# First X spreads on ScalarE's queue, and the offset-weight sums moved behind the first norm's root

## The chip, the cores and the metric

The kernel runs on one core of a Trainium2 chip. The metric is the device time of one execution in microseconds, the median of several runs. TensorE (PE) multiplies into PSUM, VectorE (DVE), ScalarE (ACT) and GpSimd (POOL) do the elementwise work, and SyncE (SP) issues nearly all transfers. All data are 32-bit floats. In the tables of the profile a product of 32-bit floats appears as two matmul instructions.

## The reference, cut to what matters

Two layers follow each other. Layer 0 is a residual bottleneck with three convolutions and batch norms over 64 images of 1024 channels, 14 by 14. Layer 1, where the change lies, is a deformable bottleneck:

```
a   = relu(group_norm(conv1x1(x, w1)))          # 1024 -> 256 channels ("first norm")
om  = conv3x3(a, w_off) + b_off                 # 27 channels: 9 x-offsets, 9 y-offsets, 9 masks
s   = bilinear_sample(a, grid + offsets) * sigmoid(mask)   # 9 taps
h   = relu(group_norm(einsum(s, w2)))
out = relu(group_norm(conv1x1(h, w3)) + x)
```

## The kernel before

**Pairs.** Layer 1 works on 32 pairs of images; a pair is one row of 392 pixels for each channel. The stages of neighbouring pairs are interleaved so that TensorE always has a product to run. `fill` (L2188) opens the layer with the first three pairs, `slot` (L1971) goes on from there, `steady` runs pairs 2 to 29 and `tail` ends it.

**Sampling as products.** The bilinear weights of an output pixel split into a factor along rows and a factor along columns. Both are computed on 126 partitions (9 taps by 14 positions) by `factors` (L1362), stored to a small DRAM tensor `wd`, and read back by transfers that repeat them: `spread_rows` (L1441) brings S, `spread_columns` (L1456) brings X, each to 126 partitions (9 image rows by 14 columns). `corners` (L1500) multiplies S by X on DVE at L1511. The product is the matrix that `sampling` (L1515) multiplies with the transposed activations `aT` at L1531. ACT copies each result from PSUM at L1539. The nine taps are split in two sets, e = 0 with five and e = 1 with four, and each set in three pieces of output rows, so a pair has six S transfers and six X transfers. `lend` (L1414) copies parts of `aT` by two more transfers.

**The opening.** The steps of `fill` are, in the order written: the first convolution of pair 0; that of pair 1 with the first norm of pair 0, `offset_weights` (L879, which makes four sums and differences of the offset weights from `goff` in DVE instructions at L883 to L888), the offset convolution of pair 0 (L1300) and `selection(0)` (L1333, which brings the offsets to the 126 partitions) among it; the transposes of pair 0; the statistics of pair 1's norm, the residual of pair 2 and `factors(0)`; the step `spread` (six S, six X and the two lends of pair 0); and then the first convolution of pair 2 (L1151), with the scale of pair 1's norm, its four relus on ACT (L1235), pair 1's shifted sums (`transform`, L1276), `sums_of_second(0, 3)` (eight DVE instructions at L916), `corners(0, 0)` and pair 1's offset convolution among it. TensorE's order is exactly that order.

**What orders the other engines.** In the opening only TensorE's order is fixed by hand. The order of DVE, ACT, POOL and SP is made by the framework's planner, which takes the ready instruction that was written first, by its own idea of the times. An instruction wrapped in `tc.keep_in_program_order` stays behind the instruction that was written just before it *for the same engine*; this ties order alone and adds no wait for a result. The first norm is three steps: `mean`, `root` (its last instruction is a power on POOL, L1062, after DVE's L1061) and `scale` (DVE, L1078 to L1085, the first of them tied). The relus of a first norm (L1235), the sums at L916 and the corners at L1511 are tied too. A transfer counts as an instruction of the engine that issues it. The framework also gives every transfer that SP or ACT issues one of eight completion semaphores in turn, and a transfer waits until the one before it on its semaphore has landed.

Of the kernel before, what the change touches and what calls it, by code (L numbers as in the profile page):

```python
# [12 lines left out]
ALU = mybir.AluOpType  # L13
# [31 lines left out]
def kernel(  # L45
# [18 lines left out]
    nc = tc.nc  # L64
# [814 lines left out]
    def offset_weights():  # L879
        g0, g1, g2 = (goff.rearrange("p (n k) o -> p n k o", k=3)[:, :, k] for k in range(3))  # L880
        w1, w0, w2, w3 = (woff_sb[:, n] for n in range(4))

        nc.vector.tensor_tensor(w0, g0, g2, ALU.add)  # L883
        nc.vector.tensor_scalar(w0, w0, 0.5, None, ALU.mult)
        nc.vector.scalar_tensor_tensor(w1, g1, 0.5, w0, ALU.mult, ALU.add)
        nc.vector.scalar_tensor_tensor(w2, g1, -0.5, w0, ALU.mult, ALU.add)
        nc.vector.tensor_scalar(w0, g0, -1.0, None, ALU.mult)
        nc.vector.tensor_copy(w3, g2)  # L888
# [41 lines left out]
    def build_second_bottleneck(l1, path, run, early):  # L930
# [160 lines left out]
        def start(p):  # L1091
            pairs[p] = {"y": Y[p % 4]}
# [189 lines left out]
        def offset_conv(p):  # L1282
            q = pairs[p]
            half = W // 2

            def step(n):

                c, k = divmod(n, 3)
                k = (1, 0, 2)[k]
                if n == 0:  # L1290

                    q["po"] = ps_d.tile([P, N2], FP, tag="pd0", name=f"om_{p}")[:, :HW].rearrange(
                        "p (i q) -> p i q", i=2
                    )
                u = room(p)

                o0, o1 = (half if k == 0 else 0), (H - 1 if k == 2 else H) * half
                i0 = o0 + (k - 1) * half
                for m in range(4):
                    nc.tensor.matmul(  # L1300
                        q["po"][ts(m, 32), :, o0:o1],
                        woff_sb[:, m, 3 * c + k, :],
                        u[:, c, (2, 0, 3, 1)[m], :, i0 : i0 + o1 - o0],
                        start=(n == 0),
                        stop=(n == 3 * MB - 1),
                    )
                if n == 3 * MB - 1:


                    om = one.tile([P, N2], FP, tag="om", name=f"om_{p}")[:32]  # L1310
                    q["sums"] = om[:, :HW], om[:, HW:]
                    even, odd = q["sums"]
                    m1, m2 = (q["po"][ts(m, 32)].rearrange("p i q -> p (i q)") for m in (0, 2))
                    nc.scalar.activation(even, m1, AF.Identity, bias=boff_sb[:32])
                    nc.vector.tensor_tensor(odd, even, m2, ALU.subtract)
                    nc.vector.tensor_tensor(even, even, m2, ALU.add)

            return [lambda n=n: step(n) for n in range(3 * MB)]
# [14 lines left out]
        def selection(p):  # L1333

            q = pairs[p]

            def step():

                if "om" not in q:
                    offsets(p)  # L1340
                om = q["om"]
                mask = one.tile([P, N2], FP, tag="om", name=f"mask_{p}")[:32]
                nc.scalar.activation(mask, om, AF.Sigmoid)
                dm = dbounce.tile([27, N2], FP, tag="dm", name=f"dm_{p}")
                nc.sync.dma_start(dm[:18], om[:18])
                nc.sync.dma_start(dm[18:], mask[18:27])
                nc.vector.tensor_reduce(
                    omax[:, p : p + 1],
                    om,
                    mybir.AxisListType.X,  # L1350
                    ALU.max,
                    apply_absolute_value=True,
                )

                wt = q["wt"] = one.tile([KY, 2, N2], FP, tag="wt", name=f"wt_{p}")
                mk = q["mk"] = one.tile([P, N2], FP, tag="om", name=f"mk_{p}")[:KY, :]
                for n, dst in ((1, wt[:, 0, :]), (0, wt[:, 1, :]), (2, mk)):
                    nc.sync.dma_start(dst, dm[ts(n, T)].unsqueeze(0).to_broadcast([H, T, N2]))

            return [step]  # L1360
# [76 lines left out]
        def sample_buffer(e, name):  # L1437
            t = one.tile([P, MB, KT[e % 2], 2, HW], FP, tag=f"sm{e % 2}", name=name)
            return t.rearrange("p c k i q -> p (c k i q)")

        def spread_rows(p, e):  # L1441

            q = pairs[p]
            k0, k1 = tapsets[e]
            S = one.tile([QR, wide * KT[e % 2]], FP, tag=f"S{e % 2}", name=f"S_{p}_{e}")
            q["S"][e] = S
            for g, r0, piece in pieces(e):
                yield nc.sync.dma_start(  # L1448
                    S[:, piece],
                    q["wd"][g][0, r0 : r0 + R, k0:k1, :]  # L1450
                    .rearrange("r k n -> r (k n)")
                    .unsqueeze(1)
                    .to_broadcast([R, W, piece.stop - piece.start]),
                )

        def spread_columns(p, e):  # L1456

            q = pairs[p]
            k0, k1 = tapsets[e]
            n = wide * KT[e % 2]  # L1460
            if shared and p < 2 and e == 0:


                first, second = (
                    one.tile([P, HB, N2], FP, tag=f"z{n}", name=f"X_{p}_{n}").rearrange("p b n -> p (b n)")
                    for n in range(2)
                )

                cut = [piece for _, _, piece in pieces(e)][-1].start
                where = lambda piece: (  # L1470
                    second[:QR, : piece.stop - cut] if piece.start == cut else first[:QR, piece]
                )

                if p == 0:
                    q["spare"] = second[:QR, wide * KT[0] - cut :]
            elif shared:
                t = sample_buffer(e, f"X_{p}_{e}")
                last = [piece for _, _, piece in pieces(e)][-1]
                spare = q.get("spare") if e == 1 else None
                where = lambda piece: (  # L1480
                    spare[:, : piece.stop - piece.start]
                    if spare is not None and piece == last
                    else t[:QR, piece]
                )
                if e == 1:
                    transformed[p + 1] = t[:, n:]
            else:
                t = one.tile([QR, n], FP, tag=f"X{e % 2}", name=f"X_{p}_{e}")
                where = lambda piece: t[:, piece]
            q["X"][e] = where  # L1490
            for g, r0, piece in pieces(e):
                yield nc.sync.dma_start(  # L1492
                    where(piece),
                    q["wd"][g][1, :, k0:k1, :]
                    .rearrange("r k n -> r (k n)")
                    .unsqueeze(0)
                    .to_broadcast([R, W, piece.stop - piece.start]),
                )
# [688 lines left out]
        def fill():  # L2187

            for p in range(3):
                start(p)  # L2190
            load_h3(2, Z0)
            steps = first_conv(0, by_inputs=True)
            norm = first_norm(0)
            steps += put(
                first_conv(1),
                norm[:3] + [offset_weights] + norm[3:] + offset_conv(0) + selection(0),
                (3, 3, 5, 5, 6, 6, 6, 6) + (12,) * (MB * 3) + (12,),
            )
            norm, (distances, end) = first_norm(1), factors(0)
            steps += [lambda: pairs[1]["gn1"].total(), lambda: residual(2, 0, 3)] + transposes(0)  # L2200

            steps += norm[:2] + [lambda: residual(2, 3, 7), distances, lambda: residual(2, 7), end]

            def spread():

                for e in range(2):
                    for n, _ in enumerate(zip(spread_rows(0, e), spread_columns(0, e))):
                        if e == n == 0:
                            lend(0)

            steps += [spread]
            steps += put(
                first_conv(2),
                norm[2:]
                + [lambda: sums_of_second(0, 3), lambda: corners(0, 0)]
                + offset_conv(1)
                + selection(1)
                + [lambda: sums_of_second(6)],
                (3, 7, 7, 8, 8, 11, 11) + (12,) * (MB * 3) + (14, 16),
            )  # L2220
            for step in steps:
                step()
# [106 lines left out]
```

## Time and profile before

| what | value |
|---|---|
| median of three runs | 2783.32 us (2782.42 to 2784.22) |
| the profiled execution | 2784.07 us, of which its span is 2782.3 us |
| busy share of the span | PE 98%, PEld 76%, DVE 85%, ACT 51%, POOL 39% |
| mean granted TensorE clock | 0.992 |
| layer 1 begins on TensorE | first L1151 matmul at 967.98 us |
| first sampling product, pair 0 | 1013.51 us |
| first product of pair 0's second convolution (L1643) | 1030.06 us |

Times are microseconds from the start of the span. In a row of the timeline the first number is the start, the second the time from there to the end of the group, then engine, line, operation, what is written and what is read, and the count; brackets give the idle time before it and what ended it. "SPq" is SP issuing a transfer: its time is the issue, not the movement of the data. Windows list the busy time of each engine in a stretch, then the granted clock, the busy share of the 16 DMA engines and the rate in GB/s.

### The profile page before, as it was taken

To read this page: it belongs to the slowest core of one execution; us is meant where nothing else is said; L and a number is where in the kernel's file an instruction comes from. 1 tells how busy PE (TensorE), PEld (TensorE's weight loads), DVE (VectorE), ACT (ScalarE), POOL (GpSimd) and SP (SyncE) were. 2 spreads that over 40 slices of the span, in tenths; PEclk is the share of its full clock that TensorE was granted. 3 is DMA by queue.
4 is the path that set the end of the run, shared out by engine and by line. 5 is a ranking of instruction groups with operands and counts; after the bars stand their busy time and mean duration, and the time that the engine had idled before them with its cause. 6 is when DMAs were issued, how large, how long until landed. Compare 5 with 4: busy or idle time off the path is not lost.

```text
span 2782.3 us, 41225 instructions
## 1 busy us (share of the span) xinstructions
PE 2717.7 (98%) x13626; PEld 2110.4 (76%) x13626; DVE 2378.3 (85%) x4856; ACT 1411.3 (51%) x2806; POOL 1092.5 (39%) x1210
## 2 busy tenths in 40 slices
PE   9999899998999989999999999999999999999997
PEld 5555555554555558889989998998899899989974
DVE  7877899998888878888888888888888888888876
ACT  0000212212555544667666767666666667576654
POOL 4631366663666402332333343333333332433221
PEclk9999999999999999999999999999999999999998
DMA  7666000002556445666757675766667666757641
GB/s 232 193 176 175 29 1 0 1 1 111 208 208 224 175 130 174 167 159 173 204 163 171 175 206 149 177 190 191 155 173 201 171 168 173 210 149 177 175 133 51
DMA packets 350324, 424.31 MB, mean 153 GB/s; under 512 B 27892, under 2 KB 292500, under 8 KB 349844
## 3 DMA queue, kind: packets, MB, share of 16 engines
q1 hardware_dynamic: 291860, 376.61, 41.3%
q0 software_dynamic: 58240, 44.96, 11.6%
q8 instruction: 110, 1.80, 0.3%
q14 instruction: 114, 0.93, 0.1%
HBM read 296.49 MB, written 116.76 MB: 149 GB/s over the span
## 4 chain that ended last, share of the span: by engine, by line
PE 56%; DVE 3%; issue 2%; DMA 2%; ACT 1%; POOL 1%; SPq 1%; ACTq 0%; DVEq 0%; POOLq 0%
PE pd L1643 21%; PE sp L1531 12%; PE d L1780 10%; PE d L1190 9%; PE om L1300 2%; DMA X<-wd 1%; PE tr L1407 1%; PE pd L1562 1%; DMA h<-in_x_dram 0%; DVE sm L1599 0%; DVE st L1013 0%; SPq L1492 0%; SPq L1448 0%; DVE h L1130 0%; DVE X L1276 0%
## 5 line engine op out<-in xcount | busy, mean ns | idle before, releaser
L1531 PE MATMUL sp<-S,aT 126*128 126x420 f32 (+3 forms) x1536 | 487.8, 416 | 7.6 <-DVE S L1511 5.2
L1643 PE MATMUL pd<-sm,w2b_sb 128*128 128x196 f32 x2232 | 400.9, 329 | 1.2 <-DVE sm L1599 1.2
L1539 ACT COPY sm<-sp 128x336 f32<-128x336 f32 (+3 forms) x640 | 283.6, 448 | 195.3 <-PE sp L1531 182.6
L1643 PEld LDWEIGHTS pd<-sm,w2b_sb 128*128 128x128 f32 x2232 | 369.6, 190 | 1.8 <-DVE sm L1599 1.8
L530 PE MATMUL c<-v,u_sb 128*128 128x392 f32 x1024 | 342.8, 497 | 11.0 <-DVE bn1sh L167 8.2
L530 PEld LDWEIGHTS c<-v,u_sb 128*128 128x128 f32 x1024 | 194.5, 191 | 159.3 <-issue 11.6
L1643 PE MATMUL pd<-sm,Sc 128*128 128x196 f32 x1674 | 303.4, 329 | 0.0
L1643 PEld LDWEIGHTS pd<-sm,Sc 128*128 128x128 f32 x1674 | 279.6, 190 | 0.2
L1599 DVE TENSOR_TENSOR sm<-sm 128x980 f32<-128x980 f32 (+2 forms) x257 | 265.2, 1051 | 12.6 <-PE pd L1643 8.8
L1531 PEld LDWEIGHTS sp<-S,aT 126*128 126x128 f32 x1536 | 259.4, 192 | 20.1 <-issue 9.5
L1867 ACT ACTIVATE z<-z,gn_0sh,gn_0sc 128x196 f32<-128x196 f32 x496 | 224.7, 536 | 12.5 <-DVE gn_0sh L1085 12.5
L1674 POOL TENSOR_TENSOR E<-V,E 128x196 f32<-128x196 f32 x31 | 18.7, 602 | 517.6 <-DVE V L1673 517.6
L516 DVE TENSOR_TENSOR v<-t 128x392 f32<-128x392 f32 x256 | 193.0, 812 | 0.0
L1780 PE MATMUL d<-h,w3b_sb 128*128 128x196 f32 x744 | 174.2, 330 | 1.6 <-ACT h L1695 1.6
L1190 PE MATMUL d<-h,w1b_sb 128*128 128x196 f32 x928 | 168.2, 329 | 1.1 <-DVE V L1206 1.1
L1780 PEld LDWEIGHTS d<-h,w3b_sb 128*128 128x128 f32 x744 | 133.0, 189 | 44.6 <-issue 18.9
L1190 PEld LDWEIGHTS d<-h,w1b_sb 128*128 128x128 f32 x928 | 155.9, 190 | 1.4 <-DVE V L1206 1.4
L385 PE MATMUL c<-xc,w1a_sb 128*128 128x392 f32 x384 | 149.1, 497 | 5.4 <-DMA xc<-in_x_dram 5.4
L1103 ACT ACTIVATE h<-h,bn3sh,bn3sc 128x392 f32<-128x392 f32 x224 | 150.0, 706 | 0.0
L1511 DVE TENSOR_TENSOR S<-S,X 126x840 f32<-126x840 f32 (+1 forms) x192 | 139.8, 767 | 9.3 <-DMA X<-wd 8.8
L504 POOL TENSOR_TENSOR t<-wpad 128x784 f32<-128x784 f32 x62 | 95.3, 1537 | 127.3 <-DVE v L516 127.3
L1792 POOL TENSOR_TENSOR E<-V,E 128x196 f32<-128x196 f32 x124 | 80.2, 647 | 159.1 <-ACT h L1103 111.3
(710 smaller groups left out, 5558.4 us busy)
## 6 DMA issues: line engine op xcount, KB each, us to landing
xc<-in_x_dram SPq DMA_DIRECT2D x128, 392.0 KB
h<-o SPq DMA_DIRECT2D x64, 784.0 KB
h<-h SPq DMA_DIRECT2D x64, 784.0 KB
out_dram<-z SPq DMA_DIRECT2D x124, 392.0 KB
h<-in_x_dram POOLq DMA_DIRECT2D x56, 784.0 KB, 12.2
X<-wd SPq DMA_DIRECT2D x64, 413.4 KB
S<-wd SPq DMA_DIRECT2D x64, 413.4 KB
S<-wd SPq DMA_DIRECT2D x64, 330.8 KB
```

What stands on the lines that cost most here:

```text
L385: nc.tensor.matmul(acc[m], a, b, start=(j == 0), stop=(j == HB - 1))
L516: nc.vector.tensor_tensor(v[:, u].rearrange("p (i y x) -> p i y x", y=7, x=7), cols[c][:, :, i : i + 13 : 2, :], cols[c][:, :, j : j + 13 ...
L530: nc.tensor.matmul(m[u], u_sb[:, c, u, k % 4, ts(o, P)], vts[k][c][:, u], start=(c == 0), stop=(c == MB - 1),)
L1103: nc.scalar.activation(y, y, AF.Identity, bias=bn3.sh[:, b : b + 1], scale=bn3.sc[:, b : b + 1])
L1190: nc.tensor.matmul(bank[:, m % 2 if m < 6 else 1], a[:, k], b[:, k], start=(k == 0 and m < 6), stop=(k == HB - 1), skip_group_check=True,)
L1511: nc.vector.tensor_tensor(S[:, piece], S[:, piece], X(piece), ALU.mult)
L1531: nc.tensor.matmul(pt[:, i], q["aT"][:, i0 + i, c, starts.index(r0), :], q["corner", e][g, r0][:, :, i0 + i, :], start=(j == 0), stop=(j = ...
L1539: nc.scalar.copy(dst, pt.rearrange("p i k n -> p k i n"))
L1599: return nc.vector.tensor_tensor(dst, a, b, ALU.subtract)
L1643: nc.tensor.matmul(bank[:, m % 2], a[:, k], b[:, k - k0],  start=(k == 0 and m in (5, 0, 2, 6)), stop=(k == T - 1), skip_group_check=True,)
L1780: nc.tensor.matmul(bank[:, m % 2 if m < 6 else 1], a, b, start=(m < 6), stop=True, skip_group_check=True)
L1867: nc.scalar.activation(z[:, ts(i, HW)], z[:, ts(i, HW)], AF.Identity, bias=n.sh[:, b, i : i + 1], scale=n.sc[:, b, i : i + 1],)
```

## The change

Two things in `fill` change; nothing else in the kernel is rewritten.

1. `spread_columns` gets a parameter for the queue, SP by default; `fill` passes ScalarE's. So the six X transfers of pair 0 are issued by ACT, and the six S transfers and the two lends stay on SP. The other 31 pairs keep all on SP.
2. `offset_weights` is written between `root` and `scale` of pair 0's first norm instead of after `scale`, and its first instruction (L883) is tied to that place by `keep_in_program_order`.

```diff
-        nc.vector.tensor_tensor(w0, g0, g2, ALU.add)
+        tc.keep_in_program_order(nc.vector.tensor_tensor(w0, g0, g2, ALU.add))
...
-        def spread_columns(p, e):
+        def spread_columns(p, e, queue=nc.sync):
...
-                yield nc.sync.dma_start(
+                yield queue.dma_start(
...
-                norm[:3] + [offset_weights] + norm[3:] + offset_conv(0) + selection(0),
+                norm[:2] + [offset_weights] + norm[2:] + offset_conv(0) + selection(0),
...
-                    for n, _ in enumerate(zip(spread_rows(0, e), spread_columns(0, e))):
+                    for n, _ in enumerate(zip(spread_rows(0, e), spread_columns(0, e, nc.scalar))):
```

## The prediction, made before the changed kernel was run

> **What bounds the kernel now.** I read the page's engine shares first, then windows over the opening, then the waits there, then the timeline of each engine. The page says that TensorE sets the time: what TensorE loses in the opening is lost at the end, since after 1030 us it hardly idles.
>
> ```profile
> PE 2717.7 (98%) x13626; PEld 2110.4 (76%) x13626; DVE 2378.3 (85%) x4856; ACT 1411.3 (51%) x2806; POOL 1092.5 (39%) x1210
> ```
>
> TensorE's own timeline, 1003 to 1031 us, shows the stretch that the change can move:
>
> ```profile
> 1003.42 3.56 PE L1151 MATMUL d<-h,w1b_sb 128*128 128x392 f32 x10 [0.57 <-ACT h L224]
> 1006.91 2.11 PE L1300 MATMUL om<-X,woff_sb 128*32 128x196 f32 x48
> 1008.95 2.90 PE L1151 MATMUL d<-h,w1b_sb 128*128 128x392 f32 x8
> 1013.51 4.04 PE L1531 MATMUL sp<-S,aT 126*128 126x420 f32 x16 [1.66 <-DVE S L1511]
> 1019.94 10.28 PE L1531 MATMUL sp<-S,aT 126*128 126x420 f32 x32 [2.40 <-DVE S L1511]
> ```
>
> Two gaps, 1.66 and 2.40 us, both waiting for corners. DVE's rows name what the corners waited for: the first came straight after the sums at L916 (their last row starts at 1011.51 and lasts 0.54) plus 0.37, the third for an X transfer.
>
> ```profile
> 1012.42 1.03 DVE L1511 TENSOR_TENSOR S<-S,X 126x840 f32<-126x840 f32 x1 [0.37 <-DMA S<-wd]
> ...
> 1018.76 1.03 DVE L1511 TENSOR_TENSOR S<-S,X 126x840 f32<-126x840 f32 x1 [1.80 <-DMA X<-wd]
> ```
>
> Three windows show the transfers' rate before and in the second gap, and the clock behind it:
>
> ```profile
> 1012.00:1017.60 5.60, 4.04 (x16) 2.53 (x16) 3.12 (x9) 2.41 (x5) 0.00 (x0) 1.00 0.59 217
> 1017.60:1019.90 2.30, 0.00 (x0) 0.00 (x0) 1.10 (x2) 0.00 (x0) 0.00 (x0) 1.00 0.58 223
> 1019.90:1023.70 3.80, 3.76 (x6) 1.70 (x7) 3.79 (x10) 2.05 (x5) 0.00 (x0) 0.55 0.59 227
> ```
>
> The rate stands near 220 GB/s (the column after the DMA share, 0.58) as long as S and X move. And the 2.3 us gap was followed by 3.8 us at clock 0.55, which stretched the eight matmuls of piece three from about 2.8 us (8 at 0.35 apart) to 4.4.
>
> SP's rows show whether issuing or moving is the limit:
>
> ```profile
> 1004.73 0.78 SPq L1492 DMA_DIRECT2D X<-wd  x1
> 1006.01 0.76 SPq L1448 DMA_DIRECT2D S<-wd  x1
> ...
> 1015.75 0.73 SPq L1492 DMA_DIRECT2D X<-wd  x1
> ```
>
> Issuing ends at 1016.5; the last X is used at 1025.43, after a wait. The six S and six X are 3.56 MB, the lends 0.26; at 220 GB/s that is 17.4 us, and traffic begins at 1007.0: it must end at 1024.4 whoever issues. Moving is the limit.
>
> Last, ACT, the new issuer, and SP's waits in the same stretch:
>
> ```profile
> 1002.76 0.61 ACT L224 ACTIVATE h<-h,bn3sh 128x392 f32<-128x392 f32 x1
> 1003.96 0.99 ACT L1235 ACTIVATE a<-a,gn_1sh,gn_1sc 128x196 f32<-128x196 f32 x2 [0.59 <-DVE gn_1sh L1085]
> ```
>
> ```profile
> SPq L1345 <- DMA S<-wd: 0.3, 1, 0.3
> ```
>
> The last row is a transfer (`dm`) that waits for an S it has nothing in common with: the rule of eight semaphores at work.
>
> **Part 1, the X transfers.** Removed: six issues of 0.74 us from SP. That is worth nothing by itself, since moving is the limit. Added: six issues on ACT, and a new order. In the order written, the last ACT instruction before pair 1's first relu (L1235) is now the sixth X. That relu is tied, so all four relus now queue behind six issues; with them wait `transform`, the offset convolution of pair 1 and all of TensorE behind it, and the sums at L916 and the corners, tied behind `transform` on DVE.
>
> An ACT-issued transfer is in no row. Nearest are SP's 0.73 to 0.78 for the same shape: I take 0.78. Bounds: 0.27 (the small `dm` issue at 1020.91) and 1.5 (each waiting out one of SP's); a gain is excluded, since it is added to a tied queue. X0 needs the `wd` store that released it at 1004.73; it can't go earlier except by part 2. Six in a row at 0.78 end at 1009.4.
>
> But the semaphores hold some back. The trace's mixed S and X order lets me suppose that the planner alternates the queues: X0 S0 X1 lend X2 lend X3 S1 X4 S2 X5. Then X4 waits for X0 to land and X5 for X1. By the half-microsecond slices of the transfer view X0 begins to move at 1007.0, 2.3 us after its issue, and has some 0.25 MB of its 0.42 across by 1008.3, when S0 joins and the 220 GB/s are halved: (0.17 + 0.14 MB)/0.11 MB per us = 2.8 us, so X1 is across at 1011.1 and lands about 0.8 later (S0 before: across between 1010.9 and 1012.2, landed by 1012.4). X5 then issues from 1011.9 to 1012.7. With part 2's 0.25 off, the relus start near 1012.45 instead of 1003.96: **8.5 late**.
>
> What follows: the sums end at 1012.05 + 8.5 = 1020.55, and the first sampling matmul comes 1.09 later (1012.42 to 1013.51): 1021.65. TensorE's side: the offset convolution idles from 1007 to about 1014.6, some 7.6 us, starts at the low clock, and with the four remaining steps ends about 1021.5, so the two meet. From there nothing is missing: S and X have all landed by some 1024.4, and the sampling runs unbroken at full clock: 4.04 + 2.82 + 5.6 (the 24 of the second set, 1024.4 to 1030.06) = 12.46. TensorE reaches L1643 at 1034.1 against 1030.06: **+4.05 us**. The low clock of before (1.6) and both gaps (4.06) are thereby given back; without that the loss would be 8.5. The next work of pair 1 (offsets to corners) has cover: its corners run at 1047.65 on DVE without a wait, and TensorE uses them at 1051.84.
>
> The Trainium skill (DMA: Bandwidth & Descriptors, Issuing engines are not separate DMA queues) says that issuing from several engines saves only the issue time, as all share the same 16 engines. It speaks against the change, and the 9.6 us between the last issue's start and its use agree: by the rule, part 1 without the queueing on ACT would be worth 0. The skill's Perfetto Trace Analysis (DMA Instruction — HWDGE) has the descriptor generator locked by one sequencer at a time; no row here shows two issuers, and by that rule alone, without the semaphores, the X issues would take turns with SP's and end near 1012.3, which by chance gives the same +4.
>
> **Part 2, the sums of the offset weights.** Six DVE instructions stood at 978.84 to 980.75, ahead of the statistics:
>
> ```profile
> 980.75 1.05 DVE L1013 BATCH_NORM_STATS2 st<-a 128x6 f32<-128x392 f32 x2
> ...
> 985.13 0.16 DVE L1078 SCALAR_TENSOR_TENSOR gn_0sc<-gn_0B,vec 128x4 f32<-128x4 f32 x1 [1.14 <-POOL gn_0B L1062]
> ```
>
> ACT's copies for the statistics start at 979.49 and take 0.85, so the statistics can start near 980.0 and end at 981.1 instead of 981.8: 0.7 gained. L883 to L887 go into the 1.14 us in which DVE waits for POOL's power; by their distances they take 0.27 + 0.27 + 0.28 + 0.38 + 0.37 = 1.57, so 0.45 sticks out. The copy at L888 depends on none of them and stays early; if it too came behind the root it would cost 0.34 more. Sum: −0.25, bounds −0.7 and +0.1. TensorE idled 0.71 before the offset convolution of pair 0 (987.86), so this is on the path down to X0's issue, and is in the 8.5 above.
>
> **Sum.** Profiled execution 2784.07 + 4.05 = 2788.1; that execution lies 0.75 above the median, so for the median 2783.32 + 4.05 = **2787.4 us**. A difference under 0.2% (5.57 us) is about what a measurement of this kernel can tell from no change, so the forecast is a small loss inside that bound.
>
> **Rivals.**
> - *Heavier hold (slower).* The sixth or fifth X gets the semaphore of S0 or a lend instead. S0 shares the rate and lands at 1012.8 to 1013.5, so the relus start at 1013.6 to 14.3 or, with issues of 1.5, near 1015: 2788.5 to 2790. It decides from a relu start of 1014, where the loss passes 5.57. For it: the `dm` row, and an alternation that I only infer. Against: X0 was ready before S0.
> - *Issues only.* No X is held: relus from 1009.2, 5.25 late; sampling from 1018.4, L1643 at 1030.85: +0.8, 2784.1. For it: if the planner sends all six before S0, they draw only on semaphores of old transfers. Even with issues of 0.27 the relus come at 1006.2, but then X3 to X5 take half the rate from S2, which lands near 1021 instead of 1018, and piece three starts near 1022: +0.6 to +2.
> - *Transfers win (faster).* Two queues raise the rate above 220 and the relus aren't late. The first corner can't precede the sums, so sampling starts at 1013.1 at best and runs unbroken: L1643 at 1025.6, −4.5, with part 2 −4.8: 2778.5 to 2783. Against it: the rate is flat while issues queue up ahead.
> - *No effect:* only part 2 shows, 2783.1.
>
> **How the numbers follow.** Forecast 0.55 (its own range 2785.8 to 2789.8, from the landing times and 0.6 to 1.1 per issue; some 0.4 of it beyond 2788.9), heavier hold 0.17 (three quarters beyond), issues only 0.20, transfers win 0.05, no effect 0.03. Slower by over 0.2%: 0.22 + 0.13 = 0.35. Faster: 0.04, since even the win stays inside and only a new planner order elsewhere could add to it. Within: 0.61. Range 2782.6 to 2791.4: below lie most of the win, above a hold with long issues.
>
> **What would show it.** Right: ACT's timeline has six X issues between 1004.5 and about 1012.5, with waits before the last two, and L1235 of pair 1 only then; TensorE idles some 7 us before the second L1300 group; the sampling then has no gap of over 0.5 us; the rate is still near 220. In part 2: L1078 with no wait for POOL, the statistics at 980.0. Wrong: relus near 1004 (the tie missed the transfer), a rate well above 220, or a gap before piece three.

## The result, and the profile after

| | median of runs | profiled execution (span) | mean clock |
|---|---|---|---|
| before | 2784.55 us (2782.11 to 2787.86, 17 runs) | 2784.07 (2782.3) | 0.992 |
| after | 2789.46 us (2786.94 to 2793.16, 17 runs) | 2789.37 (2787.6) | 0.991 |

The ratio is 1.0020, 95% interval 1.0013 to 1.0027: slower by 5.6 us (3.6 to 7.5). The prediction was 2787.4 in a range of 2782.6 to 2791.4, with "within 0.2%" as the likeliest sign. The measured loss stands at that bound.

The two profiled executions did not reach layer 1 at the same time. All positions below are therefore also given "shifted": less the difference in the start of layer 0's last twelve h updates (DVE, L213), which is 972.39 in before and 972.66 in after, so 0.27 for after.

The engine shares, on the page of the changed kernel:

```profile
PE 2719.5 (98%) x13626; PEld 2112.8 (76%) x13626; DVE 2377.9 (85%) x4856; ACT 1411.3 (51%) x2806; POOL 1093.2 (39%) x1210
```

They say nothing of the change; the opening does. TensorE's timeline there:

```profile
1003.53 3.56 PE L1151 MATMUL d<-h,w1b_sb 128*128 128x392 f32 x10 [0.93 <-ACT h L224]
1015.88 4.37 PE L1300 MATMUL om<-X,woff_sb 128*32 128x196 f32 x48 [8.79 <-DVE X L1276]
1020.18 3.60 PE L1151 MATMUL d<-h,w1b_sb 128*128 128x392 f32 x8
1023.62 11.04 PE L1531 MATMUL sp<-S,aT 126*128 126x420 f32 x44
1035.37 1.40 PE L1531 MATMUL sp<-S,aT 126*128 126x336 f32 x4 [0.70 <-ACT sm L1539]
1036.60 1.82 PE L1643 MATMUL pd<-sm,Sc 128*128 128x196 f32 x10
```

The two gaps ahead of the sampling, 1.66 and 2.40 us, are gone. A single one of 8.79 us stands ahead of the offset convolution instead, and L1643 starts at 1036.60 (shifted 1036.33) where it started at 1030.06: 6.3 us later. ACT's timeline has the reason, first as the merged rows, then the fourth and the fifth X by themselves:

```profile
1004.89 1.36 ACTq L1492 DMA_DIRECT2D X<-wd  x1
1004.93 0.55 ACT L1235 ACTIVATE a<-a,gn_1sh,gn_1sc 128x196 f32<-128x196 f32 x1
1006.35 7.55 ACTq L1492 DMA_DIRECT2D X<-wd  x5
1013.95 1.43 ACT L1235 ACTIVATE a<-a,gn_1sh,gn_1sc 128x196 f32<-128x196 f32 x3 [8.46 <-DMA X<-wd]
...
1007.96 0.84 ACTq L1492 DMA_DIRECT2D X<-wd  x1
1012.33 0.76 ACTq L1492 DMA_DIRECT2D X<-wd  x1
```

Three of the four relus stand behind the sixth X; one, tied to the copy at L1159 only, slips ahead, but `transform` starts only after the others. Between X3 (issued by 1008.80) and X4 (1012.33) ACT issues nothing for 3.5 us. In the built program X4 carries the completion semaphore that S0 has used, and X5 that of X1, which had landed by then: X5 follows X4 at once. S2, which SP issued ahead of X4, had taken the semaphore of X0. The wait list of ACT has the wait of the relus as one line; below it is SP's issue of S2:

```profile
ACT a L1235 <- DMA X<-wd: 8.5, 1, 8.5
...
1009.97 0.75 SPq L1448 DMA_DIRECT2D S<-wd  x1
```

DVE's rows show that the data of the first set were all there when the sums at L916 let the corners begin; the three corners run back to back, where before two of them waited for a transfer:

```profile
1014.97 2.28 DVE L1276 TENSOR_TENSOR X<-a 128x168 f32<-128x168 f32 x8 [9.32 <-ACT a L1235]
...
1021.17 2.33 DVE L1511 TENSOR_TENSOR S<-S,X 126x840 f32<-126x840 f32 x3
```

Windows over the transfers (granted clock, DMA share, GB/s at the end of the row):

```profile
1007.00:1012.00 5.00, 0.09 (x1) 0.00 (x0) 0.00 (x0) 0.00 (x0) 0.00 (x0) 0.94 0.62 203
1012.00:1024.30 12.30, 8.43 (x58) 5.59 (x59) 8.81 (x20) 2.33 (x5) 0.83 (x2) 0.61 0.59 222
1015.80:1021.50 5.70, 5.62 (x50) 4.07 (x51) 5.63 (x15) 0.41 (x1) 0.74 (x2) 0.50 0.59 228
```

Two queues move 203 to 228 GB/s at the same share of 0.6, as one did. And TensorE ran at half its clock (0.50 from 1015.8 to 1021.5) for the whole offset convolution and part of the four steps behind it.

Part 2 on DVE's timeline: the statistics and the scale.

```profile
980.32 1.05 DVE L1013 BATCH_NORM_STATS2 st<-a 128x6 f32<-128x392 f32 x2 [0.95 <-POOL st L988]
...
984.72 0.16 DVE L1078 SCALAR_TENSOR_TENSOR gn_0sc<-gn_0B,vec 128x4 f32<-128x4 f32 x1 [0.91 <-POOL gn_0B L1062]
...
985.63 0.15 DVE L1085 TENSOR_TENSOR gn_0sh<-gn_0sh,vec 128x4 f32<-128x4 f32 x1
```

The statistics are 0.43 earlier (0.70 shifted). But only L883 (0.35) went into the wait for POOL, of which 0.91 remain; L884 to L886 were put between L1078 and L1085, so the last instruction of the scale starts at 985.63 against 985.52 (985.36 shifted, 0.16 earlier).

### The profile page after: what moved, and what is told of

Its sections match the earlier page's. It is cut to its first block, busy times and chain, and to the rows that moved or that the text cites. A ratio compares the mean times of both kernels' runs of the same rounds, so it can differ in the third digit from the quotient of the medians.

```text
span 2787.6 us, 41226 instructions
## 1 busy us (share of the span) xinstructions
PE 2719.5 (98%) x13626; PEld 2112.8 (76%) x13626; DVE 2377.9 (85%) x4856; ACT 1411.3 (51%) x2806; POOL 1093.2 (39%) x1210
## 4 chain that ended last, share of the span: by engine, by line
PE 56%; DVE 4%; issue 2%; DMA 2%; ACT 1%; POOL 1%; SPq 0%; ACTq 0%; DVEq 0%; POOLq 0%
PE pd L1643 21%; PE sp L1531 12%; PE d L1780 10%; PE d L1190 9%; PE om L1300 2%; PE tr L1407 1%; PE pd L1562 1%; DMA X<-wd 1%; DVE sm L1599 0%; DVE st L1013 0%; DMA wt<-dm 0%; DMA S<-wd 0%; DVE h L1130 0%; DVE S L1511 0%; DMA h<-in_x_dram 0%
## 5 line engine op out<-in xcount | busy, mean ns | idle before, releaser
L1531 PE MATMUL sp<-S,aT 126*128 126x420 f32 (+3 forms) x1536 | 484.8, 414 | 4.7 <-DVE h L1676 2.6
L1643 PE MATMUL pd<-sm,w2b_sb 128*128 128x196 f32 x2232 | 400.9, 329 | 0.6 <-DVE sm L1599 0.6
L1643 PEld LDWEIGHTS pd<-sm,w2b_sb 128*128 128x128 f32 x2232 | 369.6, 190 | 1.2 <-DVE sm L1599 1.2
L1643 PE MATMUL pd<-sm,Sc 128*128 128x196 f32 x1674 | 303.4, 329 | 0.0
L1643 PEld LDWEIGHTS pd<-sm,Sc 128*128 128x128 f32 x1674 | 279.5, 190 | 0.2
L1531 PEld LDWEIGHTS sp<-S,aT 126*128 126x128 f32 x1536 | 257.8, 190 | 15.6 <-issue 6.6
L1511 DVE TENSOR_TENSOR S<-S,X 126x840 f32<-126x840 f32 (+1 forms) x192 | 139.6, 767 | 4.9 <-DMA X<-wd 4.8
```

Source lines behind the costliest of these rows:

```text
L1511: nc.vector.tensor_tensor(S[:, piece], S[:, piece], X(piece), ALU.mult)
L1531: nc.tensor.matmul(pt[:, i], q["aT"][:, i0 + i, c, starts.index(r0), :], q["corner", e][g, r0][:, :, i0 + i, :], start=(j == 0), stop=(j = ...
L1643: nc.tensor.matmul(bank[:, m % 2], a[:, k], b[:, k - k0],  start=(k == 0 and m in (5, 0, 2, 6)), stop=(k == T - 1), skip_group_check=True,)
```

## The experiments

All runs in one table. "Loss" is the ratio to the kernel before on the same chip, less one, times 2784 us, with its 95% interval; "relus" is the start of the last group at L1235 of pair 1, the corners are the second and third rows at L1511 of the first set, L1643 its first row, all in us past 1000 and shifted. The positions come from one execution each.

| kernel | loss, us | relus | corner 2 | corner 3 | L1643 |
|---|---|---|---|---|---|
| before | | 3.96 | 14.87 | 18.76 | 30.06 |
| after | 5.6 (3.6 to 7.5) | 13.68 | behind the sums | behind the sums | 36.33 |
| e1 queue only | 7.8 (4.7 to 10.9) | 13.63 | behind the sums | behind the sums | 35.64 |
| e2 sums only | -0.3 (-2.8 to 2.2) | 3.75 | 15.65 | 20.18 | 30.48 |
| e3 first four | 4.2 (1.7 to 6.7) | 8.82 | 18.56 | 20.41 | 33.35 |
| e4 behind relus | 5.0 (2.5 to 7.5) | 3.96 | 17.93 | 21.29 | 34.12 |
| e5 one queue | 3.1 (0.6 to 5.6) | 3.96 | 18.16 | 19.96 | 32.16 |
| e6 first set first | 4.2 (1.7 to 6.7) | 3.83 | 17.42 | 19.27 | 32.76 |
| e7 filled, 50 | 12.2 (8.4 to 16.1) | | | | 40.80 |
| e8 GpSimd | 11.7 (7.8 to 15.6) | 3.92 | 21.78 | 23.62 | 40.02 |
| e9 filled, 25 | 6.1 (3.6 to 8.6) | 13.55 | behind the sums | behind the sums | 36.24 |
| e10 relus late | 10.3 (6.4 to 14.2) | 14.10 | 15.97 | 21.00 | 42.48 |
| e11 lends early | 1.4 (-1.1 to 3.9) | 3.80 | 12.6 | 16.53 | 30.74 |
| e12 lends split | 3.3 (0.8 to 5.8) | 3.92 | 13.10 | 16.76 | 32.53 |

Two things limit what can be read from it. The intervals are some 2 to 4 us to each side. And before, e2 and e10 issue all S and X on SP in one and the same order, yet their second corner lies at 14.87, 15.65 and 15.97 and their third at 18.76, 20.18 and 21.00: the landing of the same transfers scatters by 1 to 2 us from one execution to the next. Only second corners later than 17 and third corners before 17 are told apart from that. That L1643 is the right place to read the loss is borne out by the table: in each run its delay against before lies within the interval of the loss.

**The two parts by themselves.** e1 is the changed kernel without the two edits around `offset_weights`; e2 is the changed kernel with this line as before:

```diff
-                    for n, _ in enumerate(zip(spread_rows(0, e), spread_columns(0, e, nc.scalar))):
+                    for n, _ in enumerate(zip(spread_rows(0, e), spread_columns(0, e))):
```

> Part 1 alone: the six X of the first pair on ScalarE's queue, the offset weights' sums where they were. Theory 'held queue' (the loss is the four relus at L1235 of pair 1 standing behind six issues on ScalarE, two of them held for a transfer that has to land): the last relus start between 1013.7 and 1014.5 us, X4 is issued some 3.5 us after X3, TensorE idles over 8 us ahead of the second L1300 group, and the time is 4.5 to 6 us above before, as with the whole change. Rival 'order' (the sums moved behind the root upset the order of layer 1's opening, and the queue costs nothing): time within 1 us of before.

> Part 2 alone: the sums of the offset weights behind the first norm's root, the X transfers on SP as before. Theory 'held queue': the relus of pair 1 at L1235 start 0 to 0.4 us earlier than 1003.96, the first X at 1004.4 to 1004.8, the two gaps of TensorE before the corners stay (about 1.7 and 2.4 us), L1643 comes at 1029.6 to 1030.2, and the time differs from before by -0.7 to +0.1 us, which the runs can't tell from none. Rival 'order': 4 us or more above before.

e1 has the whole loss, e2 none that can be told. In e2 the relus start at 1003.75 shifted, 0.21 earlier than before; in the changed kernel the first X is issued at 1004.62 shifted against 1004.73, in e1 at 1004.73. So part 2 is worth 0.1 to 0.2 us up to there, and everything else is part 1.

**Fewer issues, and the issues behind the relus.** In e3 only X0 to X3 go on ScalarE's queue; in e4 all six do, but are written as a step of their own behind the relus of pair 1. Both, and e5, e6 and e8 below, are made from the kernel before, without part 2.

```diff
# e3
-                    for n, _ in enumerate(zip(spread_rows(0, e), spread_columns(0, e))):
+                    for n, _ in enumerate(zip(spread_rows(0, e), spread_columns(0, e, lambda e, m: nc.scalar if 3 * e + m < 4 else nc.sync))):
# e4: held[e] is spread_columns(0, e, nc.scalar), begun in spread() without an issue
                 norm[2:]
+                + [lambda: [list(held[e]) for e in range(2)]]
                 + [lambda: sums_of_second(0, 3), lambda: corners(0, 0)]
```

> Part 1 for the first four X only: X0 to X3 on ScalarE's queue, X4 and X5 on SP's; offset weights as before. In the built program none of these four waits for a transfer of this stretch. Theory 'held queue': four issues of 0.77 (the first 1.36) end near 1008.8, the last relus start there, 4.9 us late instead of 10; the sums end near 1017, sampling starts near 1018.1 and then lacks nothing, L1643 at 1030 to 1032, time 0 to 2 us above before. Rival 'second queue' (two queues at once make the S and X land later, and the relus don't matter): as with all six, 4.5 to 6 us above before.

> The six X on ScalarE's queue, but written behind the four relus of pair 1 instead of ahead of them; offset weights as before. The holds of the last two X stay, only the relus no longer stand behind them. Theory 'held queue': the relus start at 1003.9 to 1004.2 as in before, TensorE has no 8 us gap and its second L1300 group takes about 2.1 us at full clock; the transfers start some 1.5 us later than before, the sums end near 1012 to 1013; what stands behind X5 now is ScalarE's copy of pair 1's offsets (L1314), which has cover. Time -1 to +2 us against before. Rival 'second queue': 4.5 to 6 us above before, with the corners waiting for X or S.

This was the surprise. e4 does what it was made for: relus at 1003.96 to the hundredth, no idle time ahead of the offset convolution. It loses 5.0 us (2.5 to 7.5) all the same. Its TensorE timeline has three gaps, each before a corner:

```profile
1006.91 2.11 PE L1300 MATMUL om<-X,woff_sb 128*32 128x196 f32 x48
1008.95 2.90 PE L1151 MATMUL d<-h,w1b_sb 128*128 128x392 f32 x8
1013.23 3.09 PE L1533 MATMUL sp<-S,aT 126*128 126x420 f32 x8 [1.38 <-DVE S L1513]
1018.49 1.19 PE L1533 MATMUL sp<-S,aT 126*128 126x140 f32 x8 [2.17 <-DVE S L1513]
1022.47 10.79 PE L1533 MATMUL sp<-S,aT 126*128 126x420 f32 x30 [2.79 <-DVE S L1513]
```

(L1533 is L1531 of the other kernels.) DVE's corners say what they waited for, and SP's row shows the third S issued only at 1012.13, after a hold of 2.7 us; before it was issued at 1010.22:

```profile
1012.14 1.03 DVE L1513 TENSOR_TENSOR S<-S,X 126x840 f32<-126x840 f32 x1 [0.36 <-DMA S<-wd]
1017.93 0.45 DVE L1513 TENSOR_TENSOR S<-S,X 126x280 f32<-126x280 f32 x1 [4.76 <-DMA S<-wd]
1021.29 1.03 DVE L1513 TENSOR_TENSOR S<-S,X 126x840 f32<-126x840 f32 x1 [2.90 <-DMA S<-wd]
...
1012.13 0.75 SPq L1448 DMA_DIRECT2D S<-wd  x1
```

X1, X2 and X3 were issued from 1006.24 on, the last of them at 1007.84, ahead of S1 (1008.64), and X4 at 1010.11, ahead of S2. X3 and X4 belong to the second set. With the rate fixed, an estimate from it is that 0.42 MB for X2 and 0.34 MB for X3 at 220 GB/s make S1 and S2 up to 3.5 us later; the corners came 3.1 and 2.5 us later. The hold of S2 is a second reason for the third corner, and this run does not part the two. The old order on one queue was the order of need. In e3, with half the queueing on ACT (relus 4.9 late), L1643 is 3.3 late: behind the relus stands again a wait for S, 1.47 and 1.40 us on its second and third corner. TensorE's own longest wait there, 1.43 us, is for a sampled copy on ACT, which stands behind the mask, and the mask behind offsets that DVE makes after the third corner. Nor does e3 part the relus from the order: of the two X left on SP the planner put one, of the second set, ahead of everything (1003.50, or 1004.66 shifted), and S2 was held for 1.6 us until an X had landed. Its profiled execution was also its fastest, 2784.12 us against a median of 2788.0. So both rivals of these two runs were half right: by its own timeline the relus cost the changed kernel its time, but taking their delay away uncovers a second loss of about the same size. In the changed kernel that one is hidden, as its corners show no wait.

**Order or queue.** Three runs on the second loss (code shortened). e5 has everything on SP in a written order; e6 has X0 to X2 on ScalarE behind the relus and the rest on SP, with S0 to S2 tied in their order; e8 has all six X on GpSimd's queue.

```diff
# e5
+                for kind, e in [("X",0),("S",0),("X",0),("L",0),("X",0),("X",1),("S",0),("S",0),("X",1),("X",1),("S",1),("S",1),("S",1)]:
+                    lend(0) if kind == "L" else tc.keep_in_program_order(next(make[kind][e]))
# e6
+                held[0] = spread_columns(0, 0, nc.scalar)      # written behind the relus
+                for s, x in zip(spread_rows(0, 1), spread_columns(0, 1)): pass
# e8
-                    for n, _ in enumerate(zip(spread_rows(0, e), spread_columns(0, e))):
+                    for n, _ in enumerate(zip(spread_rows(0, e), spread_columns(0, e, lambda e, m: nc.gpsimd))):
```

> Nothing on ScalarE's queue: all twelve spreads and the two lends on SP as before, but tied in the order in which run e4_behind_relus issued them over two queues: X0 S0 X1, the lends, X2 X3 S1 S2 X4 X5 S3 S4 S5 (X3 to X5 and S3 to S5 belong to the second set). New theory 'order of need' (the rate is fixed near 220 GB/s, so X2 and X3 ahead of S1 and S2 make the corners of the first set late, whichever queue issues them): relus at 1004 us as before, second corner (the 0.45 us row of DVE) at 16.5 to 18 past 1000 instead of 14.87, third at 20.5 to 21.5 instead of 18.76, L1643 at 1033 to 1034.5 instead of 1030.06, time 2.5 to 5 us above before. Rival 'second queue' (two queues at once disturb one another, the order is nothing): corners and L1643 within 0.7 us of before, time within 1 us. Times within the profile are read against the start of layer 0's last twelve h updates, 972.39 in before.

> X0 to X2 on ScalarE's queue behind the four relus of pair 1, everything else on SP: two queues are used, but nothing of the second set, except X3, which the planner puts first on SP, stands ahead of the first set. Theory 'order of need': relus at 1004, third corner at 18 to 19.7 past 1000, L1643 at 1029.3 to 1031, time within 1.5 us of before. Rival 'second queue': as in e4_behind_relus, third corner near 1021, L1643 near 1034, time 3 to 5 us above before.

> The six X of the first pair on GpSimd's queue, which nobody of this stretch stands behind and which has semaphores of its own; offset weights as before. Theory 'order of need': relus at 1004 as before, but all X compete with S0 to S2, so the corners come 1 to 3 us late and L1643 at 1031 to 1034; time 1 to 4 us above before, with the rate still at 200 to 245 GB/s. Rival 'ScalarE alone was the trouble': corners and L1643 as before or up to 3 us earlier if the third queue raises the rate above 245 GB/s; time -3 to +1 us.

e5's second corner is at 18.16, 2.2 to 3.3 us later than in the three executions with the old order, on one queue. So the order alone delays a corner and, with L1643 at 32.16 and a loss of 3.1 (0.6 to 5.6), the sampling. Its rows (0.97 later than shifted), and a window over the slow part of its sampling; the last line is such a window for e4:

```profile
1019.13 0.45 DVE L1511 TENSOR_TENSOR S<-S,X 126x280 f32<-126x280 f32 x1 [2.81 <-DMA S<-wd]
...
1014.49 3.09 PE L1531 MATMUL sp<-S,aT 126*128 126x420 f32 x8 [1.66 <-DVE S L1511]
1019.68 1.19 PE L1531 MATMUL sp<-S,aT 126*128 126x140 f32 x8 [2.11 <-issue]
1022.11 11.19 PE L1531 MATMUL sp<-S,aT 126*128 126x420 f32 x32 [1.23 <-DVE S L1511]
...
1022.00:1027.70 5.70, 5.59 (x8) 2.83 (x9) 4.11 (x10) 1.53 (x3) 0.00 (x0) 0.51 0.34 130
...
1022.40:1028.00 5.60, 5.53 (x8) 2.47 (x8) 5.50 (x16) 1.82 (x4) 0.00 (x0) 0.50 0.21 75
```

The late corner costs in two ways. The gaps of TensorE ahead of the corners add up to 5.0 us in e5 and 6.3 in e4, against 4.06 in before. And behind the last gap TensorE ran some 5.6 us at half its clock in both, where before ran 3.8 us at 0.55; from these rows I estimate 1.1 us more. So about half of e5's 2.1 us at L1643, and a quarter of e4's 4.1, is clock and not waiting. e5's third corner (19.96, no later than the old order gave in e2 and e10) and L1643 came earlier than forecast. One reason is that e5 copied e4's order not quite: X4 is ahead of S2 in e4 and behind it in e5, and e5's S2 was not held by a semaphore. e6 went against the theory: it should have been within 1.5 us and lost 4.2 (1.7 to 6.7), with the second corner at 17.42, though its third, 19.27, lay where the theory had it. Here the planner put X3 first on SP, and X1 and X2 ran beside S0 and S1; and behind its third corner TensorE waited 1.94 us for a copy on ACT. That two queues do harm beyond the order is not excluded: e5, e4 and e6 lie within each other's intervals. What is shown is that the order is enough for a loss on a single queue. e8 has the latest corners, and a surprise on GpSimd:

```profile
1004.73 3.81 POOL L1492 DMA_DIRECT2D X<-wd  x6 [5.27 <-DMA wd<-wt]
1008.52 1.08 POOL L1280 COPY X<-a 128x56 f32<-128x56 f32 x2
...
1010.00:1016.00 6.00, 4.05 (x38) 2.12 (x30) 1.50 (x3) 0.90 (x2) 0.00 (x0) 1.00 1.03 214
...
1016.52 1.03 DVE L1511 TENSOR_TENSOR S<-S,X 126x840 f32<-126x840 f32 x1 [5.00 <-DMA S<-wd]
```

I had written that nobody stands behind GpSimd's queue; `transform` has two copies there (L1280), which waited out the issues and held the offset convolution for 1.98 us. The DMA engines were busy all the time (share 1.03 instead of 0.6) and moved no more, 214 GB/s; and the first S landed 4 us late. Yet TensorE's longest wait there, 5.92 us, was again for a sampled copy on ACT behind the mask; the corners themselves cost it 3.56, so e8's loss is not the order alone.

**The low clock.** Idle matmuls on TensorE ahead of the offset convolution of the changed kernel, into its accumulator, 50 in e7 and 25 in e9:

```diff
+                if early and p == 1 and n == 0:
+                    for _ in range(25):
+                        nc.tensor.matmul(q["po"].rearrange("p i q -> p (i q)"), w1b_sb[:, 0, :P], pairs[2]["y"][:, 0, :HW], start=True, stop=True)
```

> The changed kernel with 50 idle matmuls (128x196, 0.17 us each at full clock, some 8.3 us, results never used) written on TensorE ahead of the offset convolution of pair 1, into its own accumulator: TensorE stays busy while it waits for the relus. Theory 'low clock on the path': the second L1300 group takes about 2.1 us instead of 4.37 and the eight L1151 behind it 2.9 instead of 3.60, so TensorE is ready near 1021; sampling then starts at DVE's first corner, near 1022.2 instead of 1023.6, L1643 1.2 to 1.6 us earlier than in the changed kernel, time 1 to 1.6 us below it. Rival 'the corners bind alone': L1643 within 0.3 us of the changed kernel.

> As e7_filled, with 25 idle matmuls instead of 50: in e7 each took 0.335 us, two passes of 0.17, so that 50 of them kept TensorE busy 7 us too long; 25 take 8.4 us, as long as the idle time of the changed kernel. Results of the idle matmuls are never used. Theory 'low clock on the path': second L1300 group about 2.1 us instead of 4.37, the eight L1151 2.9 instead of 3.60; sampling starts at DVE's first corner, near 1022.2 instead of 1023.62; L1643 1.2 to 1.6 us earlier than in the changed kernel, both read against the start of layer 0's last twelve h updates; time 1 to 1.6 us below it. Rival 'the corners bind alone': L1643 within 0.3 us of the changed kernel.

e7 was sized wrong and held TensorE until 1023.05; it still gave one number: 12.74 us of sampling (1027.83 to 1040.57, a wait of 0.27 in it) when all data are there and the clock is full. In e9 the filling fits:

```profile
1006.67 8.46 PE L1297 MATMUL om<-h,w1b_sb 128*128 128x196 f32 x50
1015.55 2.67 PE L1309 MATMUL om<-X,woff_sb 128*32 128x196 f32 x48 [0.42 <-DVE X L1276]
1018.15 2.90 PE L1151 MATMUL d<-h,w1b_sb 128*128 128x392 f32 x8
1022.01 3.56 PE L1540 MATMUL sp<-S,aT 126*128 126x420 f32 x12 [0.96 <-DVE S L1520]
1026.45 6.25 PE L1540 MATMUL sp<-S,aT 126*128 126x140 f32 x24 [0.88 <-ACT sm L1548]
1033.49 2.98 PE L1540 MATMUL sp<-S,aT 126*128 126x112 f32 x12 [0.79 <-ACT sm L1548]
```

(Lines from L1295 on stand nine later here.) The granted clock is 1.00 from 1006.7 to 1021.1, the second L1300 group takes 2.67 and the eight L1151 2.90 again, and sampling starts 1.4 us earlier, shifted, as the theory said. But L1643 comes at 36.24 against 36.33, and the loss is that of the changed kernel, 6.1 (3.6 to 8.6). The gain went into two waits, 0.88 and 0.79 us, for sampled copies on ACT: in ACT's order the mask of pair 1 (L1343 in before) and the distances (L1371) stand among those copies, and they wait for DVE. In the changed kernel the low clock is real and off the path that sets the end. The rival named the right size for a wrong reason: it is ACT's order that binds, not the corners.

**Late relus alone.** e10 is the kernel before with 18 idle copies on ACT ahead of the relus, tied:

```diff
+                for _ in range(18):
+                    tc.keep_in_program_order(nc.scalar.copy(idle, pairs[2]["y"][:, CB - 1, :]))
```

> The kernel before, no transfer changed, with 18 idle copies (128x392, results never used) on ScalarE where the changed kernel has its six X issues, so that the last relus of pair 1 come some 9 us late by themselves. Theory 'late relus are the whole loss' (the order of the transfers costs nothing once the sums come after them): with relus at 1013 to 1014, sums to 1020 to 1021, TensorE idle some 8 us and its clock low after it, sampling unbroken, L1643 5 to 6.5 us later than before as in the changed kernel, time 4 to 6 us above. Rival 'both add' (the disordered transfers cost something on top in the changed kernel): L1643 2 to 4 us later than before, time 1.5 to 3.5 us above.

It failed as a test. Relus at 14.10 were as wanted, but the planner now put half of `transform` behind the third corner, which waited 4.58 us for X2, so TensorE idled 15.88 us instead of 8.79. What late relus alone cost with the transfers in the old order stays open. That they are enough for the loss in the changed kernel is argued from its corners without a wait. e10 gives the unbroken sampling once more: 12.61 us.

**A version that beats both?** If 0.26 MB less ahead of the corners are worth 1.2 us, the lends can go where SP has nothing to do. e11 writes them behind the transposes; e12 also writes the third corner behind pair 1's offsets.

```diff
# e11
-            steps += [lambda: pairs[1]["gn1"].total(), lambda: residual(2, 0, 3)] + transposes(0)
+            steps += [lambda: pairs[1]["gn1"].total(), lambda: residual(2, 0, 3)] + transposes(0) + [lambda: lend(0)]
...
-                        if e == n == 0:
-                            lend(0)
# e12, on top
-                + [lambda: sums_of_second(0, 3), lambda: corners(0, 0)]
+                + [lambda: sums_of_second(0, 3), lambda: corners(0, 0, 0, 1)]
...
+                + [lambda: corners(0, 0, 2), lambda: sums_of_second(6)],
-                (3, 7, 7, 8, 8, 11, 11) + (12,) * (MB * 3) + (14, 16),
+                (3, 7, 7, 8, 8, 11, 11) + (12,) * (MB * 3) + (14, 15, 16),
```

> The kernel before, all on SP, with the two lends of the first pair (aT to aT, 0.26 MB) written right behind the transposes that they copy from, instead of behind S0: SP has nothing to issue from 997.2 to 1002.5, and what they copy is there by 995.3. Theory 'order of need': 0.26 MB less ahead of the corners at 220 GB/s is 1.2 us: second corner at 13.5 to 14.2 past 1000 instead of 14.87, third at 17.4 to 18.0 instead of 18.76, the 2.40 us gap of TensorE down to 1.0 to 1.7, L1643 1 to 2 us earlier than 1030.06, time 0.5 to 2 us below before, on the edge of what the runs can tell. Rival 'issue or sums bind': third corner and L1643 within 0.4 us of before.

> e11_lends_early with the third corner of the first set written behind pair 1's offsets (L1331) and their largest value (L1347) instead of ahead of them. In e11 the third corner came 2.2 us earlier than in before, but TensorE then waited 1.94 us for a sampled copy on ScalarE (L1539), which stood behind the mask (L1343), which waited 3.39 us for L1331 behind that corner. Theory 'the offsets are next': the mask comes at 16.5 to 17.5 past 1000, the 1.94 us wait is gone, L1643 at 1027.5 to 1028.8 against 1030.74 in e11 and 1030.06 in before (read against layer 0's last h updates), time 1 to 3 us below before. Rival 'the second set's data bind anyway': L1643 at 1029.7 or later, time within 1 us of before.

The transfers did what was forecast and more: third corner at 16.53 and 16.76, 2 us or more earlier than in any kernel with the lends behind S0. TensorE's timeline shows where that went, e11 first, then e12:

```profile
1017.78 0.94 PE L1531 MATMUL sp<-S,aT 126*128 126x420 f32 x2 [0.95 <-DVE S L1511]
1020.66 8.93 PE L1531 MATMUL sp<-S,aT 126*128 126x420 f32 x28 [1.94 <-ACT sm L1539]
...
1024.51 1.37 PE L1531 MATMUL sp<-S,aT 126*128 126x336 f32 x4 [0.46 <-DVE S L1511]
1030.13 2.45 PE L1531 MATMUL sp<-S,aT 126*128 126x336 f32 x4 [4.25 <-ACT sm L1539]
```

```profile
1019.81 0.53 ACT L1343 ACTIVATE mask<-off 32x392 f32<-32x392 f32 x1 [3.39 <-DVE off L1331]
...
1028.98 0.86 ACT L1371 ACTIVATE wt<-wt 126x784 f32<-126x784 f32 x1 [5.00 <-DVE wt L1370]
```

In e11 the sampled copies stand behind the mask, which waits for DVE; with that mended in e12, they stand behind the distances of pair 1, which wait for their transfer. Each time a wait on the path was shortened, the next instruction in ACT's fixed order took it up. Neither beats the kernel before: 1.4 (-1.1 to 3.9) and 3.3 (0.8 to 5.8).

## Why the prediction was right, point by point

The number was right, and the size nearly: 2787.4 forecast, 2789.46 measured, in the range. But the execution fell in the rival "heavier hold" (2788.5 to 2790), not in the likeliest case. Of the signs named, the order of issue, TensorE's idle time and the rate came true; a wait stood before the fifth X only, one gap of 0.70 us lay in the sampling, and L1078 still waited for POOL.

- **Relus behind the issues: right in kind, short by 1.2 us.** Forecast 1012.45, measured 1013.68 shifted, for three of the four relus. The order X0 S0 X1 lend X2 lend X3 S1 came out as supposed, but then S2 stood ahead of X4 (issued at 1009.97 and 1012.33) and took the semaphore of X0; so X4 was held by S0 and not by X0, and X5, which had X1's as forecast, was held by nothing more. That is the rival's semaphore, and its relu start of 1013.6 to 14.3 holds the measured one. Issues took 0.76 to 0.84, as taken from SP's rows, and the first 1.36.
- **TensorE's idle time and clock: right in kind, mis-sized.** 7.6 us forecast, 8.79 measured. TensorE was ready at 1023.35 shifted, not 1021.5, so it and the corners did not meet: the first corner was done near 1022. The 1.9 us are the later relus (1.2 us) and a low clock that cost more than the sum had it. As e9 shows, that term moved nothing at the end.
- **Sampling unbroken: right.** 12.46 forecast; 12.98 measured with the wait of 0.70 in it, 12.74 and 12.61 in e7 and e10.
- **L1643 +4.05: measured +6.3.** Of this, 1.2 never reached the end: 22 sampling matmuls near 2700 us, partly at a low clock in both, took 9.05 us in before's profiled execution and 7.82 in after's. The spans differ by 5.3, the medians by 4.9.
- **"Moving is the limit whoever issues": right on the rate, wrong in what was drawn from it.** By it, a second queue without the queueing on ACT was worth 0, and "issues only" +0.8. e3 comes nearest to that case, with four issues and none of them held (but with S2 held, see above): 4.2 us (1.7 to 6.7), L1643 3.3 late. e4 had no relu queueing at all and lost 5.0. The step that failed is the price of the order: the sum let all transfers end at 1024.4 in either kernel, which they nearly did, but the first set has to be there by 1018.8, and which transfer goes first was given no term in it; only the rival "issues only" had one, X3 to X5 delaying S2, at +0.6 to +2. This did not touch the number, since in the changed kernel no corner waited for a transfer.
- **The Trainium skill, DMA: Bandwidth & Descriptors (Issuing engines are not separate DMA queues):** that a second issuer brings issue time alone, and no bandwidth, is borne out by the 203 to 228 GB/s. Perfetto Trace Analysis (DMA Instruction — HWDGE) has the generator locked for one sequencer at a time; that whole issues take turns, as the prediction drew from it, is not borne out here. X2 was issued from 1007.16 to 1007.92 beside a lend on SP from 1006.97 to 1007.88, each in its usual time. A lock over a part of the issue is not excluded.
- **Part 2: near in size, but not by the way forecast.** -0.25 forecast, -0.1 to -0.2 measured on the path to X0. The statistics gained what was forecast; but four of the five sums found another place than the wait for POOL, of which 0.91 us stayed.
- **The other rivals.** "Transfers win" and "no effect" fall: the rate is unchanged, and e1 has the loss.

## What to carry to other kernels

A transfer that is issued from a computing engine is an instruction of that engine: everything tied behind it waits for its issue and for whatever its semaphore waits for, so look at which instruction comes next there before you move one. Where the rate is the limit, a second queue does not move more, it changes the order; price the order by what each consumer needs first, and not by when the last byte lands. And where one engine's fixed order (here ACT's copies from PSUM among masks and distances) is nearly critical, a wait that is shortened elsewhere can come back there, as it did in e9, e11 and e12.

## What was not expected of the hardware

- The first transfer on ScalarE's queue took 1.36 us to issue, the next ones 0.76 to 0.84; where SP issued another X at the same moment (e3, e6), the first took 1.58 and 1.63, and SP's stayed at 0.78 to 0.79.
- Six X on GpSimd's queue were issued in 3.81 us, 0.64 each, and kept all 16 DMA engines busy (share 1.03 against 0.6 for the same transfers from SP or ScalarE) at an unchanged 214 GB/s.
- After 8.79 us without work TensorE's clock stood at 0.50 from 1015.8 to 1021.5 while it was busy; with idle matmuls in the gap (e9) it stood at 1.00 for the offset convolution and the four steps.
- The same transfers in the same order land some 2 us apart in three executions (third corners at 18.76, 20.18 and 21.00), while the relus of e4 and before start at the same hundredth (1003.96).
